# A decoder layer in float32 on one core: queries and gates of the cross attention by seven products, another order of the steps into and out of the experts

## The chip, the core and the metric

The kernel runs on one core of one Trainium2 chip. The metric is the device time of one execution in microseconds (us). The five engines of a core are named as the profile names them: PE (TensorE, with PEld its weight loads), DVE (VectorE), ACT (ScalarE), POOL (GpSimd) and SP (SyncE, which here only issues transfers). PE takes a product of float32 as two instructions.

## What is computed

A decoder layer on x (8 x 112 tokens, 512 wide) and a context (8 x 375 x 512), all float32:

```
x = layernorm(x + self_attention(x))          # 16 heads of 128, causal
q, k = feature_map(x Wq^T), feature_map(ctx Wk^T)   # where(x > 0, x + 1, exp(x))
gate = sigmoid(x Wg^T + bg)
attn = (q . sum(k v)) / (q . sum(k) + 1e-6)    # 16 heads of 32
x = layernorm(x + (attn * gate) Wo^T)
logits = x router^T + bias                     # 8 experts, the top 2 with softmax weights
out = sum over the 2: w_e * (act(x gate_up_e + b) down_e + b)
x = layernorm(x + out)
```

Here act is `(clip(up, -7, 7) + 1) * g * sigmoid(1.702 g)` with `g = min(gate, 7)`.

## The kernel before

Tokens lie in seven tiles of 128 (`xn`), weights in nine slabs of 128 x 4 x 512 (`slab`; three more come for the experts). Up to 445 us the self attention runs: per head, `seven` (L319) makes queries and keys for both halves of the tokens by seven products in place of eight, from sums of tokens (`combine_tokens`, L302, on DVE) and sums of weights (`combine_weights`, L312, on POOL). The products share three PSUM banks, ACT and DVE take intermediate results out between them.

Then come two pairs of context blocks (`project_pair`, L797), the transposes of the tokens (`transposing`, L210) and, from 470 to 518 us, queries and gates of the cross attention (L923 to L942): two weights, four groups of 128 columns, two halves of 448 tokens, four chunks, 64 products. DVE and ACT form the feature map (L261) out of PSUM, ACT the sigmoid. After that `biases` and `more_biases` (L943 to L949) are cleared by POOL, and the sums of the next pair are made there (L788).

The order of the instructions on PE, DVE, ACT and SP is that of the text only inside `manual_schedule` (L478, and L1142 to the end); elsewhere, and always on POOL, a planner orders them by priorities. From L1143 a loop over the 8 batches does the attention (`summarize`, `attend`), and chains of generators lie beside it: `tick()` (L727) moves each chain by one `yield`, `settle(n)` runs them until n are left. `close(t)` (L1045) is such a chain: output projection, normalisation, routing of tile t (`route`, L556), and, for some t, `list_blocks` (L642), which works out which expert each step takes and which block of 128 tokens. `LISTS` (L40) has five lists: steps 0; 1 and 2; 3 and 4; and the two lists of the rest, both after the last tile. Each tile's tokens are scattered to `store` in DRAM by POOL.

18 steps follow (L1366): fetch 128 tokens (`fetch_tokens`, L1031, POOL queue), transpose, two inner products (`products`, L1127, 512 columns each of gate and up), activation (`project`, L1208), transpose, down product (`down`, L1231), result `y` scattered to `parts` in DRAM. `LANES` says in which slabs a step's weights lie; steps 5 to 12 take two half blocks. `fetch_inner`, `fetch_down` issue the weights on the SP queue, behind what that queue waits for; `fetch_biases` (L1014) brings bias rows on the ACT queue (steps 0 and 1: SP) to every 32nd partition, and `spread_biases` (L1026) copies them to the others by `stream_shuffle` on DVE.

The end: after step 12's scatter the two results of each token are read back (L1426, 14 loads on SP), added and normalised by `close_tiles` (L1297). The blocks of the last five steps (`LATE`) are not ready by then: they gather the other result (`gather`, L1273), add their own (`add_own`, L1270, POOL for three of them), and are normalised and written by row numbers (`write`, L1282). Rows that occur in later blocks too are found by `find_again` (L1327), and step 17 takes step 16's rows by a product with a 0/1 matrix (`finish`, L1350).

Of the kernel before, what the change touches and what calls it, by code (L numbers as in the profile page):

```python
# [48 lines left out]
LISTED = [*range(EARLY), *range(10, 18), *range(EARLY, 10)]  # L49
LATE = 5  # L50
# [10 lines left out]
def decoder_layer(ctx: ExitStack, tc: tile.TileContext, t_in: dict, out: bass.AP):  # L61
# [170 lines left out]
    def closing_roots(a: int, b: int):  # L232
        rstd = closing[:, 2, a:b]
        nc.scalar.activation(rstd, closing[:, 1, a:b], AF.Sqrt, bias=eps)
        nc.vector.reciprocal(rstd, rstd)
        nc.vector.scalar_tensor_tensor(
            closing[:, 3, a:b], closing[:, 0, a:b], -1.0, rstd, ALU.mult, ALU.mult
        )
# [48 lines left out]
    with tc.tile_pool(name="att", bufs=2) as att:  # L287
# [14 lines left out]
        def combine_tokens(a: int, b: int):  # L302
# [16 lines left out]
        def seven(name: str, tag: str, w1, w2, ws, cols, turned_: bool, c11, c12, c21, c22):  # L319
# [236 lines left out]
    def route(t: int):  # L556

        x2T = side.tile([P, C, P], F32, tag="x2T", name=f"x2T_{t}")
# [165 lines left out]
    xblk = [side.tile([P, W], F32, name=f"xblk{i}") for i in range(NQ)]  # L724
# [12 lines left out]
    with tc.tile_pool(name="cross", bufs=2) as cr:  # L737
# [179 lines left out]
        wxo = weights("wxo", 0, 8)  # L917
# [5 lines left out]
        for n, w in (("xq", wxq), ("xg", wxg)):  # L923
            for g in range(C):
                for half in range(2):
                    cols = slice(half * HALF, (half + 1) * HALF)
                    ps = bank(f"{n}ps_{g}_{half}")
                    for c in range(C):
                        nc.tensor.matmul(  # L929
                            ps[:, :HALF],  # L930
                            w[:, c, g * P : (g + 1) * P],
                            xT[:, c, cols],
                            start=(c == 0),
                            stop=(c == C - 1),
                        )
                    if n == "xq":
                        tmp = cr.tile([P, HALF], F32, tag="tmp", name=f"qt_{g}_{half}")
                        feature_map(qf[:, g, cols], ps[:, :HALF], tmp)
                    else:
                        nc.scalar.activation(  # L940
                            gate[:, g, cols], ps[:, :HALF], AF.Sigmoid, bias=bg[:, g : g + 1]
                        )  # L942
# [3 lines left out]
        more_biases = side.tile([P, 2 * D], F32, name="more_biases")  # L946
# [67 lines left out]
        def fetch_biases(s: int, queue=nc.scalar, engine=ET.Activation):  # L1014

            for i in range(len(LANES[s])):
                on, half = part_of(s, i)
                e = listed(0, s, half, engine, E - 1)
                for to, of in ((inner_bias(s), gubs), (down_bias(s), t_in["db"])):
                    to_ = to[on.start : on.stop : XH]  # L1020
# [5 lines left out]
        def spread_biases(s: int):  # L1026

            for b in (inner_bias(s), down_bias(s)):
                nc.vector.stream_shuffle(b, b, [0] * XH)  # L1029
# [15 lines left out]
        def close(t: int):  # L1045
# [12 lines left out]
            for i, (n, steps_) in enumerate(LISTS):  # L1058
                if t == n - 1:
                    list_blocks(i)  # L1060
# [66 lines left out]
        def products(s: int, st, k: int):  # L1127

            ps = st["ps", k] = bank(f"gups_{s}_{k}")
            for c in range(C):  # L1130
# [12 lines left out]
        for b in range(B):  # L1143
# [6 lines left out]
            else:  # L1150

                fetch_inner(1, of=(1,))
                for s in range(2):
                    fetch_biases(s, nc.sync, ET.SP)
                fetch_down(1)
                fetch_inner(2)
                sums = summarize(b)
# [4 lines left out]
                products(0, steps[0], 1)  # L1162
                tick()
                steps.append(start(1, cr, "bdkv"))
                spread_biases(0)
                last = close(NT - 1)
                next(last)
                settle(0)
# [3 lines left out]
                products(1, steps[1], 1)  # L1172
# [22 lines left out]
    with tc.tile_pool(name="moe", bufs=2, reuse_waits="tile") as moe:  # L1195
# [12 lines left out]
        def project(s: int, st, k: int):  # L1208

            if s > 1:  # L1210
                products(s, st, k)
# [19 lines left out]
        def down(s: int, st):  # L1231
            ps = bank(f"yps_{s}", "aux")
            for c in range(C):
                for rows_, q in parts_of(s):
# [4 lines left out]
                        start=(c == 0),  # L1239
                        stop=(c == C - 1 and s < STEPS - 1),  # L1240
                    )
            if s == STEPS - 1:
                finish(ps, st)
                return
            y = st["y"]
# [246 lines left out]
```

## Time and profile before

| | |
|---|---|
| median of 3 runs | 957.3 us (953.56 to 959.45) |
| the profiled execution | 954.05 us, span 952.5 us, clock 0.986 |
| queries and gates | 470.15 to 518.26 us |
| first expert product | 702.71 us |
| last down product begins | 927.87 us |
| row writes of the late blocks | 939.91 to 946.18 us |

The page gives the busy time of each engine and the span in 40 slices. In the answers, a line of the timeline has the start, the time in all, the engine, the line in the kernel, the operation, output and input, their shapes, the number of instructions, and in brackets how long the engine was idle before and what released it. A line of the chain has start, length and what ran. A line of the waits has who waited, for whom, the total, how often, and the longest. Several instructions merged into one line show their time together.

### The profile page before, as it was taken

Reading aid. Unit: us, or ns where it says so; the run is one execution under the profiler, and the core shown is the slowest. Engines: PE = TensorE matmul, PEld = TensorE weight load, DVE = VectorE, ACT = ScalarE, POOL = GpSimd, SP = SyncE. Lnnn points to the kernel's source line nnn. Section 1 sums busy time; section 2 is a strip of 40 time slices with the busy share of each in tenths; the row PEclk is TensorE's granted clock in tenths of the full one; section 3 lists DMA queues with packets and bytes.
Section 4 is the critical chain, followed back from the end, with each engine's and each line's share of the span. In section 5 each row is a group of like instructions: output and inputs, shape, how many; then the busy total and the mean of one; then the engine's idle time right before and its main releaser. Section 6 shows DMA issues by size and latency. Waiting matters only on the chain.

```text
span 952.5 us, 11049 instructions
## 1 busy us (share of the span) xinstructions
PE 907.8 (95%) x3915; PEld 463.2 (49%) x3915; DVE 500.7 (53%) x1094; ACT 252.8 (27%) x439; POOL 203.0 (21%) x265
## 2 busy tenths in 40 slices
PE   8999999999999999999999999999998899999981
PEld 4346655664445654664555445455454443334440
DVE  5115451663123551457430567666678765555795
ACT  2213321332102330332322232323323322222232
POOL 3103310311001321302002212222101342222343
PEclk9999999999999999999999999999998999999996
DMA  9998201000221001021100111110476999868943
GB/s 331 378 329 283 89 1 44 1 1 1 72 105 44 1 1 44 1 91 62 33 1 1 33 33 56 54 56 1 167 268 232 394 372 330 299 240 347 380 174 130
DMA packets 34919, 130.48 MB, mean 137 GB/s; under 512 B 3846, under 2 KB 8006, under 8 KB 25136
## 3 DMA queue, kind: packets, MB, share of 16 engines
q1 hardware_dynamic: 29184, 114.06, 32.9%
q0 software_dynamic: 4768, 14.98, 4.4%
q10 hardware_dynamic: 912, 0.74, 0.3%
q8 instruction: 31, 0.51, 0.2%
q14 instruction: 24, 0.20, 0.1%
HBM read 122.02 MB, written 30.06 MB: 160 GB/s over the span
## 4 chain that ended last, share of the span: by engine, by line
PE 77%; DVE 12%; DMA 6%; ACT 2%; issue 2%; POOL 1%; ACTq 0%; POOLq 0%; SPq 0%; DVEq 0%
PE ops L272 10%; PE gups L1132 9%; PE yps L1235 4%; PE zps L456 3%; PE xqps L929 3%; PE xgps L929 3%; PE sps L408 2%; PE xops L272 2%; DVE z L902 2%; PE vps_3a L330 1%; PE vps_2a L330 1%; PE pps L448 1%; PE vps_0a L330 1%; PE vps_1a L330 1%; DMA slab<-in_wg_dram 1%
## 5 line engine op out<-in xcount | busy, mean ns | idle before, releaser
L1132 PE MATMUL gups<-slab,bT 128*64 128x512 f32 (+1 forms) x416 | 131.1, 596 | 0.0
L272 PE MATMUL ops<-slab,zT 128*128 128x512 f32 x224 | 98.1, 593 | 0.0
L1132 PEld LDWEIGHTS gups<-slab,bT 128*64 128x64 f32 (+1 forms) x416 | 47.7, 157 | 66.0 <-issue 64.9
L314 POOL TENSOR_TENSOR ws<-slab 128x256 f32<-128x256 f32 x16 | 12.2, 761 | 275.9 <-PE qk_9c L330 83.0
L1235 PE MATMUL yps<-slab,aT 128*64 128x512 f32 (+1 forms) x208 | 68.2, 605 | 0.9 <-ACT aT L1083 0.9
L272 PEld LDWEIGHTS ops<-slab,zT 128*128 128x128 f32 x224 | 41.9, 190 | 49.3 <-issue 48.6
L1214 DVE TENSOR_TENSOR gu<-gups,biases 128x512 f32<-128x512 f32 x36 | 24.8, 689 | 58.6 <-PE gups L1132 58.6
L1083 ACT COPY aT<-aT_ps 128x512 f32<-128x512 f32 x18 | 10.5, 584 | 131.3 <-PE aT_ps L1079 122.6
L281 DVE TENSOR_TENSOR xn<-xn,ops 128x512 f32<-128x512 f32 x28 | 19.1, 684 | 46.2 <-PE ops L272 46.2
L1235 PEld LDWEIGHTS yps<-slab,aT 128*64 128x64 f32 (+1 forms) x208 | 24.8, 161 | 38.4 <-issue 35.7
L463 DVE COPY zT<-zps 128x448 f32<-128x448 f32 x32 | 20.0, 624 | 39.8 <-PE zps L456 39.8
L456 PEld LDWEIGHTS zps<-pT,v 112*128 112x128 f32 x256 | 33.5, 192 | 12.3 <-issue 11.2
L432 DVE TENSOR_REDUCE nm<-p 112x4 f32<-112x448 f32 x32 | 19.7, 616 | 30.5 <-POOL p L422 30.5
L456 PE MATMUL zps<-pT,v 112*128 112x112 f32 x256 | 33.4, 273 | 0.0
L1248 POOL DMA_INDIRECT parts<-y,nums x16 | 17.2, 1073 | 65.2 <-DVE y L1246 38.8
L272 PE MATMUL xops<-slab,gate 128*128 128x512 f32 x56 | 25.7, 602 | 4.8 <-DVE gate L904 4.8
L1029 DVE STREAM_SHUFFLE biases<-biases 128x1024 f32<-128x1024 f32 (+1 forms) x28 | 29.9, 1103 | 0.0
L618 POOL DMA_INDIRECT store<-xn,rows x14 | 14.4, 1030 | 71.7 <-DVE cmp L660 40.1
L416 ACT ACTIVATE p<-sps 112x448 f32<-112x448 f32 x32 | 17.4, 544 | 45.6 <-PE sps L408 45.6
L408 PE MATMUL sps<-k,q 128*112 128x112 f32 x256 | 28.0, 262 | 0.0
L434 ACT ACTIVATE p<-p 112x448 f32<-112x448 f32 x32 | 18.4, 576 | 33.3 <-DVE p L433 32.2
L408 PEld LDWEIGHTS sps<-k,q 128*112 128x112 f32 x256 | 26.6, 178 | 0.5 <-issue 0.4
(807 smaller groups left out, 1705.2 us busy)
## 6 DMA issues: line engine op xcount, KB each, us to landing
slab<-in_wg_dram SPq DMA_DIRECT2D x26, 1024.0 KB
slab<-in_wu_dram SPq DMA_DIRECT2D x26, 1024.0 KB
slab<-in_wd_dram SPq DMA_DIRECT2D x26, 1024.0 KB
store<-slab SPq DMA_DIRECT2D x8, 1806.0 KB
cT<-in_ctxT_dram SPq DMA_DIRECT2D x8, 750.0 KB
slab<-in_wq_dram SPq DMA_DIRECT2D x4, 1024.0 KB
slab<-in_wk_dram SPq DMA_DIRECT2D x4, 1024.0 KB
slab<-in_wo_dram SPq DMA_DIRECT2D x4, 1024.0 KB
```

Of the source, the lines that this page charges most:

```text
L272: nc.tensor.matmul(ps, aT[:, c, t * P : (t + 1) * P], w[:, c, :], start=(c == 0), stop=(c == C - 1),)
L281: nc.vector.tensor_add(xn[:, t, :], xn[:, t, :], ps)
L330: nc.tensor.matmul(ps[:rows, :n], l[:, c, :], r[:, c, :], start=start and c == 0, stop=c == C // 2 - 1, skip_group_check=not start,)
L408: nc.tensor.matmul(ps[:S, i * S : (i + 1) * S], qk["q"][:, rows], qk["k"][:, rows], start=True, stop=True,)
L432: nc.vector.tensor_reduce(nm, p, AX.X, ALU.max, negate=True)
L456: nc.tensor.matmul(zps[:, i * S : (i + 1) * S], v[:, half * 4 + i, hl * DH : (hl + 1) * DH], pT[:, i * S : (i + 1) * S], start=True, stop= ...
L463: nc.vector.tensor_copy(zT[:, hl, half * HALF : (half + 1) * HALF], zps[:, :HALF])
L929: nc.tensor.matmul(ps[:, :HALF], w[:, c, g * P : (g + 1) * P], xT[:, c, cols], start=(c == 0), stop=(c == C - 1),)
L1029: nc.vector.stream_shuffle(b, b, [0] * XH)
L1132: nc.tensor.matmul(ps[rows_], st["bT"][:, c, rows_], slab[3 * q + k][:, c, :], start=(c == 0), stop=(c == C - 1),)
L1214: nc.vector.tensor_add(a, ps, st["bias"][:, k * I : (k + 1) * I])
L1235: nc.tensor.matmul(ps[rows_], st["aT"][:, c, rows_], slab[3 * q + 2][:, c, :], start=(c == 0), stop=(c == C - 1 and s < STEPS - 1),)
```

## The change

1. Queries and gates use `seven`, with its token sums (`x1s`) in a new tile `tokens` and its weight sums in slab 8. One group gives 128 columns of the queries and of the gates for both halves. The results go to SBUF, and feature map and sigmoid work there in place, the sigmoid for two groups at a time over 896 columns. The load of `wxo` into slab 8 stands after the products.
2. `tokens` holds the four token blocks (`xblk`), `more_biases` and the transposed tile of `route`, which were tiles of their own.
3. Steps 0, 1, 16 and 17 (`SPREAD`) load their bias rows to all 128 partitions and are not spread by DVE. For steps 0 and 1 the loads go behind step 1's down weights and step 2's inner weights on SP.
4. In the last batch, `settle(0)` (routing of tile 5, list 2) stands before `close` of the last tile; lists 3 and 4 come one `yield` later. `products` can do part of its chunks: those of (0, 1), (1, 1) and (2, 1) are cut in two around other work.
5. At the end `close_tiles` begins a step's half sooner and stops at other places, ACT scales all seven tiles, the three additions on POOL move to DVE, the three late blocks are closed before step 17's down product, the product with `same` opens that product's bank, and a block's row write follows its scaling. `find_again` stands after `down`.

```diff
@@
     def closing_roots(a: int, b: int):
         rstd = closing[:, 2, a:b]
         nc.scalar.activation(rstd, closing[:, 1, a:b], AF.Sqrt, bias=eps)
+        yield
...
-        x2T = side.tile([P, C, P], F32, tag="x2T", name=f"x2T_{t}")
+        x2T = tokens[:, NQ * W + 2 * D :].rearrange("p (c n) -> p c n", c=C)
...
-    xblk = [side.tile([P, W], F32, name=f"xblk{i}") for i in range(NQ)]
+    tokens = side.tile([P, NQ * W + 3 * D], F32, name="tokens")
+    xblk = [tokens[:, i * W : (i + 1) * W] for i in range(NQ)]
...
-        wxo = weights("wxo", 0, 8)
+        ws = slab[8].rearrange("p c n -> p (c n)").rearrange("p (i n) -> p i n", i=2)
+        ws = [ws[:, i].rearrange("p (a c n) -> p a c n", a=4, c=C // 2) for i in range(2)]
+        group = [slice(g * P, (g + 1) * P) for g in range(C)]
+        for g in range(2):
+            combine_weights(ws[g], wxq[:, :, group[g]], wxg[:, :, group[g]])
+        x1s = tokens[:, : 4 * T].rearrange("p (a c n) -> p a c n", a=4, c=C // 2)
...
+        combine_tokens(0, HALF, x1s)
+        halves_ = slice(0, HALF), slice(HALF, T)
+        for g in range(C):
+            for _ in seven(
+                f"xqg_{g}", "mm", wxq[:, :, group[g]], wxg[:, :, group[g]],
+                [ws[g % 2][:, i] for i in range(4)], slice(0, HALF), False,
+                qf[:, g, halves_[0]], qf[:, g, halves_[1]],
+                gate[:, g, halves_[0]], gate[:, g, halves_[1]], x1s, x1ends,
+            ):
+                pass
+            if g + 2 < C:
+                combine_weights(ws[g % 2], wxq[:, :, group[g + 2]], wxg[:, :, group[g + 2]])
+            for half, cols in enumerate(halves_):
+                tmp = cr.tile([P, HALF], F32, tag="tmp", name=f"qt_{g}_{half}")
+                feature_map(qf[:, g, cols], qf[:, g, cols], tmp)
+            if g % 2:
+                for i in (g - 1, g):
+                    nc.scalar.activation(
+                        gate[:, i, :], gate[:, i, :], AF.Sigmoid, bias=bg[:, i : i + 1]
+                    )
+        wxo = weights("wxo", 0, 8)
...
-                    to_ = to[on.start : on.stop : XH]
+                    to_ = to[on] if s < SPREAD or s >= STEPS - SPREAD else to[on.start : on.stop : XH]
...
                 if t == n - 1:
+                    if i == 3:
+                        yield
                     list_blocks(i)
...
-                for s in range(2):
-                    fetch_biases(s, nc.sync, ET.SP)
                 fetch_down(1)
                 fetch_inner(2)
+                for s in range(SPREAD):
+                    fetch_biases(s, nc.sync, ET.SP)
...
-                products(0, steps[0], 1)
+                products(0, steps[0], 1, range(2))
                 tick()
+                products(0, steps[0], 1, range(2, C))
                 steps.append(start(1, cr, "bdkv"))
-                spread_biases(0)
+                settle(0)
                 last = close(NT - 1)
                 next(last)
-                settle(0)
                 chains.append(last)
                 products(1, steps[1], 0)
                 tick()
-                products(1, steps[1], 1)
+                products(1, steps[1], 1, range(2))
...
         def close_tiles():
             for t in range(NT):
                 engine = nc.vector if t < 4 else nc.gpsimd
                 engine.tensor_add(xn[:, t, :], xn[:, t, :], seconds[:, t, :])
                 closing_stats(t, xn[:, t, :])
-                if t in (1, 2):
+                if t in (0, 2, 4):
                     yield
+            roots = closing_roots(0, NT)
+            next(roots)
             yield
-            closing_roots(0, NT)
+            for _ in roots:
+                pass
+            yield
             for t in range(NT):
-                closing_scale(t, xn[:, t, :], t > 2)
+                closing_scale(t, xn[:, t, :], True)
                 nc.sync.dma_start(out=out[t * P : (t + 1) * P, :], in_=xn[:, t, :])
-                if t == 2:
-                    yield
+                if t == 1:
                     yield
...
+        def end_steps(*several, by_act=()):
+            for _ in closing_roots(at_close(several[0]), at_close(several[-1]) + 1):
+                pass
+            for s in several:
+                closing_scale(at_close(s), steps[s]["sum"], s in by_act)
+                write(steps[s])
...
             if st:
                 project(s, st, 0)
-                if s < STEPS - 1:
-                    tick()
+                tick()
+                if s == 0:
+                    products(1, steps[1], 1, range(2, C))
+                if s == 2:
+                    products(2, st, 1, range(2))
...
                 gate_sigmoid(s, st)
+                if s == STEPS - 1:
+                    tick()
                 begin_result(s)
...
             if s == STEPS:
+                two = steps[STEPS - 2]
+                ps = before_["begun"] = bank("yps_last", "aux")
+                nc.tensor.matmul(ps, before_["same"], two["y"], start=True, stop=False)
+                three = range(STEPS - LATE, STEPS - 2)
                 settle(0)
-                close_steps(*range(STEPS - LATE, STEPS - 2), by_act=True)
+                for i in three[1:]:
+                    add_own(i)
+                    stats_of(i)
+                add_own(STEPS - 2)
+                end_steps(*three, by_act=three)
+                add_own(STEPS - 1)
+                stats_of(STEPS - 2)
...
-            if STEPS - LATE <= s < STEPS - 1:
-                find_again(s + 1)
-            if s + 1 < STEPS:
+            if 0 < s < STEPS - 1:
                 spread_biases(s + 1)
             if before_:
                 down(s - 1, before_)
+            if STEPS - LATE <= s < STEPS - 1:
+                find_again(s + 1)
             if s == STEPS - 1:
-                for late in steps[STEPS - LATE : STEPS - 2]:
-                    add_own(late, nc.gpsimd)
-                add_own(before_)
-                add_own(st)
-            if before_:
+                add_own(STEPS - LATE)
+                stats_of(STEPS - LATE)
+            if before_ and s < STEPS - 1:
                 if s == STEPS - 3:
                     chains.append(close_tiles())
-                if s != STEPS - 3:
-                    tick()
+                tick()
...
             if s == STEPS:
-                for st in steps[STEPS - LATE :]:
-                    write(st)
+                stats_of(STEPS - 1)
+                end_steps(STEPS - 2, STEPS - 1)
```

## The prediction

> **What bounds the kernel now.** I read the page, the table by stretches, the waits of TensorE, the timeline of the two places where TensorE idles, and the chain of the end. The page, with the DMA share per slice in its last line:
>
> ```profile
> span 952.5 us, 11049 instructions
> ...
> PE 907.8 (95%) x3915; PEld 463.2 (49%) x3915; DVE 500.7 (53%) x1094; ACT 252.8 (27%) x439; POOL 203.0 (21%) x265
> ...
> DMA  9998201000221001021100111110476999868943
> ```
>
> TensorE is busy 95%, so only removed products and its idle stretches pay. The table by stretches (stretch, its length, busy time of PE, PEld, DVE, ACT, POOL, granted clock, DMA share, GB/s):
>
> ```profile
> 470.00:518.00 48.00, 48.00 (x131) 24.40 (x130) 10.86 (x18) 10.83 (x17) 0.00 (x0) 1.00 0.00 0
> ...
> 720.00:740.00 20.00, 16.69 (x50) 8.78 (x48) 17.42 (x90) 7.07 (x12) 4.36 (x5) 0.83 0.81 315
> 740.00:760.00 20.00, 17.03 (x53) 8.51 (x53) 14.21 (x33) 8.58 (x14) 8.12 (x9) 1.00 1.01 393
> 780.00:800.00 20.00, 20.00 (x88) 7.00 (x84) 11.36 (x24) 3.23 (x6) 6.70 (x9) 1.00 1.01 372
> ...
> 905.00:925.00 20.00, 18.45 (x55) 8.66 (x52) 19.23 (x45) 4.64 (x8) 7.50 (x8) 1.00 0.47 176
> 925.00:952.50 27.50, 5.95 (x16) 2.16 (x14) 14.62 (x27) 8.53 (x14) 11.06 (x10) 0.71 0.38 134
> ```
>
> Three places count: the queries and gates, 48 us of TensorE alone; the passage into the expert steps, 6.3 us idle at 720 to 760 with VectorE busy; the end, where VectorE has 19.23 of 20 us. The waits of TensorE (total, times, longest):
>
> ```profile
> PE aT_ps L1079 <- DVE gu L1223: 5.7, 3, 3.0
> ...
> PE yps L1352 <- DVE y L1246: 1.9, 1, 1.9
> PE keys L1332 <- DVE sums L1392: 1.6, 1, 1.6
> ```
>
> VectorE is what TensorE waits for. The timeline shows why at the end:
>
> ```profile
> 927.61 2.50 POOL L1271 TENSOR_TENSOR sums<-sums,y 128x512 f32<-128x512 f32 x2
> 927.61 3.74 DVE L236 SCALAR_TENSOR_TENSOR closing<-closing 128x7 f32<-128x7 f32 x1
> ```
>
> L236 on 128x7 takes 3.74 us; its two later runs took 0.16. It ends at 931.35, as GpSimd's three additions do (930.05 + 1.27): VectorE stood still while GpSimd added. The chain of the end:
>
> ```profile
> 935.09 3.74 DMA out_dram<-xn
> ```
>
> The last tile is written at 935.09 and lands at 938.83. Then GpSimd issues five row writes, 939.91 to 946.18, 1.3 us apart, and 6.3 us later the span ends.
>
> **The sum's base.** The profiled execution took 954.05 us (span 952.5). The median shown is 957.3, 3.25 more (runs 953.56 to 959.45). I work against 954.05 and add half of that, 1.6, at the end.
>
> **A, queries and gates: -3.7.** Removed: 64 products of 448 columns, each two instructions at a pitch of 0.376 us (470.15 to 518.26), 48.1 us. Added: four groups of seven products in two chunks, 56 x 0.752 = 42.1. That is -6.0. The new helpers: L307 to L310 on VectorE (0.62 for 448 columns, so some 1.1 each for 896). The transposed tokens are whole at 471.05; the second sum is ready at 473.2, when the first four products end (470.15 + 3.0): cover exact. The weight sums are 4 x 0.73 per group on GpSimd, idle for 80.6 us there; the first two groups come early, the others lie beside 10.5 us of products, as do a group's four evictions on ScalarE (0.53 each) and five operations on VectorE (0.43 to 0.62). Inside a group the third eviction stands between two products on one bank; in the same pattern at L352 a weight load waits 0.2 us, because the next group's product is put between (vps_1a at 223.96 stands between two of vps_0a): +0.2 x 4 = 0.8. At the stage's end ScalarE has, after the last product, an addition (0.6) and a minimum (0.4) on VectorE ahead, then one exponential 0.6, a table load 1.28 and two sigmoids of 896 columns, some 1.1 each: free 5.4 us on, while the eviction that kvps_2a waits for was issued 2.2 us on and needed 4.5 us on: +1.5. GpSimd's third memset (0.98, earlier at 427) comes into the same gap, covered by that wait. -6.0 + 0.8 + 1.5 = -3.7. Ends: -6.0 (all hidden); +2.0 (no filler, 4 x 0.9, second and third table load in the way, 2.6, and the wait 1.8). I take the value near the vps rows, the same code. The load of wxo moves behind the last product on SP; it has until 552.85, and the context load issued behind it at 531.7 loses nothing.
>
> **B, into the expert steps: -4.7.** From 708.46 TensorE does gups(0,1), lps, bT, xops, cps, gups(1,0), x2T, gups(1,1), lps, cps, aT, bT, yps(0), gups(2,0), aT, bT, gups(2,1): by their pitches (3.43 for eight, 0.44 for a transpose, 0.8 for lps) 28.7 us. It took 39.0 (to 747.44): 10.3 lost, namely 1.5 on cps, 1.8 and 3.0 on gu, 2.9 at a half clock (yps 731.03 to 736.5 in place of 3.43) and the rest in steps of tenths. New order on VectorE: both shuffles of steps 0 and 1 go (2.05 each: 1.29 + 0.73), route(5) and its list come ahead of tile 6's normalisation. List 2 then ends at 718.2 in place of 723.1; tile 6 is normalised at 720.9 (719.56); gu of step 0 at 727.9 (729.1); step 1's gate at 731.0, the two long lists (5.4 less 1.1 of L675, blocked as L236 was) to 735.3, gu of step 1 at 738.4 (743.0). TensorE: half of gups(1,1) covers lps, half of gups(2,1) covers gu(1). Left: 0.5 on cps(5), 2.1 on gu(0), 0.95 as aT's copy stands behind tile 6's exponential on ScalarE, 1.7 at a half clock, 0.4 small. gups(2,1) ends at 742.7: -4.7. Weights: the loads of step 3 follow list 2 on SP (723.75 to 718.8) and fill a DMA queue idle from 711.5 to 723, so the stream moves by the same 4.8; step 1's down load and step 2's loads go ahead of the two bias loads on SP, which land at some 708 and are needed at 721. Lists 3 and 4 end only 1.1 earlier, but their loads queue behind seven others. GpSimd: the scatter of tile 5 goes 5 us sooner, so tokens(3) do. Ends: -7.3 (no half clock, no copy wait); 0 (the weights hold it).
>
> The half clock in this trace came at 539.84 after a wait of 2.05 us, for 3.41 us, and at 727.6 for 6.83 us; so I let 2.1 us of idling cost 1.7, half of such a window. The Trainium skill, "TensorE: Matmul & The Clock Gate", section "HAM oscillation", only speaks of idle gaps over some 3.4 us; by that rule the 1.7 would not be lost and B would be -6.4.
>
> **C, the end: -5.2.** VectorE between step 16's first gate and step 17's: 17.7 us (905.04 to 922.7) loses step 17's shuffles 2.05, and tile 0 goes ahead (1.56) into the room of step 16's shuffles: gate of 17 at 920.4, gu at 923.6 (926.24). keys go behind yps on TensorE, so 1.6 goes and yps(16) ends at 923.8. ScalarE: root of seven at 919.3 (aT(16) behind it), sigmoid 922.1, two scales, two copies to 925.0, aT(17) 925.6, five scales at 0.73 to 929.25 (934.32). That is 5.1 sooner for the last tile's write, landing at 933.7; five row writes follow from 934.8 at 1.28 to 941: the span's end moves by 5.1 to 5.2. Beside it on VectorE: three additions (0.67) from GpSimd and five statistics, to 934.3; the last scale at 936.0 is needed by the fifth write at 939.9. So the writes are late next, and -8.0 is their end if the write of the tiles does not hold them; -2.5 if VectorE alone sets it (gu's 2.6).
>
> **D, whole bias rows for four steps: +0.3.** 128 rows of 6 KB for 4 or 8 KB: 0.77 MB a step, 2 us at 380 GB/s. For steps 0 and 1 the queue idles. Those of 16 and 17 go ahead of 14 loads of tiles on SP and of the down weights issued at 901.34, landing 905.7; yps(15) now wants them at 909.3: +0.3, ends 0 and +4.
>
> Sum: -3.7 - 4.7 - 5.2 + 0.3 = -13.3, so 940.8 beside 954.05; with the 1.6, **942.4**.
>
> **The rivals.** R1, the weights hold B: DMA share 1.0 from 740 to 800, and yps waited 1.0 us for a down load at 817.25. For: lists 3 and 4, said to come sooner, are put off by one tick and gain only 1.1 us. Against: queue idle until 723. Time 942.4 + 4.7 = 947. R2, A gives nothing: the planner spends it on table loads and bank waits: 946. R3, the change's end gains nothing, since ScalarE's root of seven waits for tiles 5 and 6, whose additions GpSimd may put behind four gathers (922.28 to 927.6) that wait for a scatter; then aT(16) is copied at 931 in place of 920 and C is +6.5: 942.4 + 11.7 = 954. Against: the three additions ran at 900.66 and 905.16. R4, slower: the token blocks, the transposed tile and biases are now one tile; if a load into one part waits for readers of the others, the prefetch goes and each of 13 steps waits some 3 us of the 8 us landing: 942.4 + 39 = 981; over 1.8 us a step it is slower than before by 1%. Against: the biases tile has its parts loaded and read at once (load at 793.73, shuffle of another part at 795.94).
>
> **How the numbers follow.** As forecast 0.50 (936 to 947); R1 0.17, R2 0.13, R3 0.14, R4 0.06. A measurement of this kernel can tell about 1%, 947.7 to 966.9, from no change. Faster: 0.50 + 0.12 + 0.09 = 0.71; same: the rest of R1 and R2, 0.09, and R3 less 0.02, 0.12: 0.21; slower 0.08. The range runs from the good ends (A -6.0, B -7.3, C -8.0, D 0: 934.4) to R3 (954), cut to 934 to 953.
>
> **What would show it.** Products xqg of 42 us and kvps_2a beside them; list 2 at some 5 us after bT(1); no wait of keys; no GpSimd addition L1271; L236 at 0.16; the last tile written some 5 us after step 17's yps begins; row writes 1.3 apart. It is wrong if wd or wg loads appear among TensorE's waits, if aT waits for ScalarE, or if the first row write waits for a scale and not for a tile.

## The result and the profile after

The changed kernel took 945.9 us (median of 4 runs, 942.5 to 949.5) beside 956.7 us for the kernel before: ratio 0.989, 95% interval 0.986 to 0.9925, so it is 10.8 us faster (7 to 13 by the interval). The forecast was 942.4 us, the range 934 to 953. Measured a second time on another occasion (experiment after_again) it took 944.2 us, ratio 0.989 (0.9857 to 0.9921).

The page of the changed kernel; its profiled execution took 949.54 us, the span is 948.0:

```profile
span 948.0 us, 11057 instructions
...
PE 908.9 (96%) x3899; PEld 462.2 (49%) x3899; DVE 506.2 (53%) x1094; ACT 273.2 (29%) x463; POOL 213.1 (22%) x278
...
DMA  8978201000041000011100211010477999768964
```

TensorE has 16 instructions (8 products) fewer and is busy 1.1 us longer, since this execution began at half clock until 13.6 us, the kernel before only until 4.5; in the repeat TensorE is busy 902.1 us. The table by stretches, with the columns as before:

```profile
470.00:518.00 48.00, 47.33 (x143) 24.15 (x142) 22.82 (x37) 25.07 (x36) 6.62 (x8) 1.00 0.00 0
720.00:740.00 20.00, 16.75 (x51) 9.09 (x50) 15.99 (x71) 9.81 (x14) 5.05 (x6) 0.83 0.97 379
740.00:760.00 20.00, 20.00 (x60) 9.82 (x59) 15.48 (x33) 5.75 (x10) 5.82 (x8) 1.00 1.01 365
905.00:925.00 20.00, 17.67 (x43) 7.82 (x42) 18.04 (x39) 7.41 (x11) 9.23 (x9) 0.91 0.55 224
925.00:948.00 23.00, 6.73 (x19) 2.74 (x17) 11.94 (x25) 9.57 (x15) 8.43 (x8) 0.72 0.45 161
```

Two things to see. From 720 to 760 TensorE now idles 3.25 us where it idled 6.3, all of it ahead of 740 and at a granted clock of 0.83. From 905 to 925 VectorE is nearly as full as before (18.04 of 20; 19.23 before) and TensorE idles more (2.3; 1.55 before). The waits of TensorE show by whom:

```profile
PE aT_ps L1107 <- DVE gu L1253: 3.3, 1, 3.3
PE yps L1265 <- DMA slab<-in_wd_dram: 2.3, 1, 2.3
...
PE kvps_2a L815 <- POOL biases L798: 1.9, 1, 1.9
```

Of the three waits for gu one is left, keys no longer wait, and step 15's down load is there, which was not. The end of the chain:

```profile
902.92 7.34 DMA slab<-in_wd_dram
910.40 5.37 PE yps L1265 x8
...
927.79 3.54 ACT xn L245 x5
931.35 2.79 DMA out_dram<-xn
```

The order of the end is the one forecast (TensorE's last product, five scales on ScalarE, the last tile's write, row writes), but it comes late, and behind a down product that ran at 5.37 us in place of 3.60.

**Where the time went.** To compare kernels I cut the span at five marks on TensorE: the first transposes of x1T, the first kvps_10a, the first gups, yps of step 1 (at 746.50 here), yps of step 14 (896.51), the end. The columns are differences of these times in each kernel's trace; the last two are the median of all its runs and its ratio to the kernel before, measured beside it.

| kernel | to x1T | to kvps_10a (A) | to gups | to yps 1 (B) | to yps 14 | to the end (C, D) | span | median | ratio (interval) |
|---|---|---|---|---|---|---|---|---|---|
| before | 467.1 | 198.5 | 37.1 | 44.7 | 150.5 | 54.5 | 952.5 | 956.7 | 1 |
| after | 471.7 | 194.1 | 38.8 | 41.9 | 150.0 | 51.5 | 948.0 | 945.9 | 0.989 (0.986-0.9925) |
| after again | 467.0 | 192.4 | 37.1 | 41.5 | 150.9 | 52.4 | 941.3 | 944.2 | 0.989 (0.986-0.992) |
| e1 | 467.6 | 198.3 | 37.1 | 41.3 | 149.8 | 51.6 | 945.7 | 947.6 | 0.994 (0.992-0.996) |
| e2 | 467.1 | 192.4 | 38.8 | 42.1 | 149.2 | 51.5 | 941.0 | 944.3 | 0.9905 (0.9885-0.992) |
| e3 | 466.8 | 194.1 | 38.8 | 41.5 | 149.7 | 51.7 | 942.5 | 943.8 | 0.9905 (0.988-0.993) |
| e4 (of before) | 467.3 | 196.6 | 37.1 | 44.9 | 150.7 | 55.2 | 951.7 | 953.9 | 0.9994 (0.997-1.0015) |
| e5 | 467.4 | 194.1 | 37.1 | 46.6 | 150.4 | 52.3 | 947.8 | 949.3 | 0.993 (0.9915-0.995) |
| e7 | 467.3 | 192.4 | 38.8 | 39.5 | 150.7 | 52.9 | 941.6 | 943.6 | 0.988 (0.984-0.991) |
| e8 | 466.8 | 194.1 | 38.8 | 42.0 | 149.9 | 51.6 | 943.2 | 944.3 | 0.988 (0.9855-0.990) |
| e9 | 467.4 | 194.1 | 38.8 | 41.6 | 150.7 | 52.2 | 944.7 | 943.8 | 0.987 (0.985-0.989) |
| e10 | 466.9 | 194.1 | 38.8 | 40.9 | 149.7 | 52.0 | 942.3 | 943.3 | 0.987 (0.984-0.991) |
| b1 | 466.9 | 194.1 | 38.8 | 39.6 | 150.7 | 51.5 | 941.5 | 943.8 | 0.987 (0.984-0.990) |
| b3 | 468.7 | 194.1 | 38.8 | 39.3 | 150.7 | 51.4 | 943.0 | 942.6 | 0.986 (0.983-0.989) |

The columns "to kvps_10a" and "to gups" hold chance: in each of them a window of 3.41 us at half clock (granted clock 0.5) falls or does not, worth 1.7 us (see the last section). Without it the change is A -4.2 to -4.4, B -2.8 to -3.3, the middle between -0.5 and +0.4, the end -2.1 to -3.0. That makes -9 to -11; the medians show -10.8, and -11.5 in the repeat (944.2 beside 955.7). Medians of kernels this close can't be told apart (their intervals are 4 to 7 us wide), so the experiments are read stage by stage.

### The profile page after: what moved, and what is told of

It reads as the page before. It is cut to its first block, busy times and chain, and to the rows that moved or that the text cites. A ratio compares the mean times of both kernels' runs of the same rounds, so it can differ in the third digit from the quotient of the medians.

```text
span 948.0 us, 11057 instructions
## 1 busy us (share of the span) xinstructions
PE 908.9 (96%) x3899; PEld 462.2 (49%) x3899; DVE 506.2 (53%) x1094; ACT 273.2 (29%) x463; POOL 213.1 (22%) x278
## 4 chain that ended last, share of the span: by engine, by line
PE 79%; DVE 10%; DMA 5%; ACT 2%; POOL 2%; issue 1%; SPq 0%; POOLq 0%; ACTq 0%; DVEq 0%
PE ops L274 10%; PE gups L1162 10%; PE yps L1265 5%; PE zps L460 3%; PE sps L412 2%; PE xops L274 2%; DVE z L907 2%; DMA biases<-in_db_dram 2%; PE vps_3a L334 1%; PE vps_2a L334 1%; PE vps_1a L334 1%; PE pps L452 1%; PE vps_0a L334 1%; DMA slab<-in_wg_dram 1%; PE kvps_2a L815 1%
## 5 line engine op out<-in xcount | busy, mean ns | idle before, releaser
L1162 PEld LDWEIGHTS gups<-slab,bT 128*64 128x64 f32 (+1 forms) x416 | 46.6, 157 | 64.7 <-issue 64.5
L1265 PE MATMUL yps<-slab,aT 128*64 128x512 f32 (+1 forms) x200 | 65.4, 614 | 2.3 <-DMA slab<-in_wd_dram 2.3
L274 PEld LDWEIGHTS ops<-slab,zT 128*128 128x128 f32 x224 | 41.9, 190 | 49.3 <-issue 49.1
L1244 DVE TENSOR_TENSOR gu<-gups,biases 128x512 f32<-128x512 f32 x36 | 24.8, 690 | 59.0 <-PE gups L1162 58.9
L274 PE MATMUL xops<-slab,gate 128*128 128x512 f32 x56 | 25.8, 604 | 4.8 <-DVE gate L909 4.8
L907 DVE RECIPROCAL z<-z 128x448 f32<-128x448 f32 x8 | 23.6, 2953 | 0.3
```

Of the source, the lines that this page charges most:

```text
L274: nc.tensor.matmul(ps, aT[:, c, t * P : (t + 1) * P], w[:, c, :], start=(c == 0), stop=(c == C - 1),)
L907: nc.vector.reciprocal(zf, zf)
L1162: nc.tensor.matmul(ps[rows_], st["bT"][:, c, rows_], slab[3 * q + k][:, c, :], start=(c == 0), stop=(c == C - 1),)
L1244: nc.vector.tensor_add(a, ps, st["bias"][:, k * I : (k + 1) * I])
L1265: nc.tensor.matmul(ps[rows_], st["aT"][:, c, rows_], slab[3 * q + 2][:, c, :], start=(c == 0 and s < STEPS - 1), stop=(c == C - 1),)
```

## The experiments

**e1, A undone.** The 64 plain products of the kernel before stand again in place of the seven-product groups.

```diff
-        for g in range(C):
-            for _ in seven(f"xqg_{g}", ...)
+        for n, w in (("xq", wxq), ("xg", wxg)):
+            for g in range(C): ...   # the 64 products of before
```

> The changed kernel with part A alone undone: queries and gates by the 64 plain products of 448 columns again. Theory (A is worth 4.45 us: products 4.3 shorter, its new wait and half clock 2.0 and 0.15, against 2.1 lost at the same place before): 945.9 + 4.4 = 950.3 us, ratio to the kernel before 0.994; the 64 products take 48.1 us and the next product waits for no memset of GpSimd. Rival (R2, A gives nothing, since what it wins is taken back by weights that come no sooner): 946 us, ratio 0.989, with the first expert products starting at the same distance from the load that feeds them.

947.6 us, ratio 0.994, as the theory had it. The A column goes back to 198.3, and nothing later takes the difference back, so R2 falls. The waits of e1 also show the trade inside A: kvps_2a's wait for GpSimd (1.9) is gone, and an old wait is back.

```profile
PE sumps L869 <- DVE kf L829: 1.8, 1, 1.8
```

**e5, B undone.** Lists, splits, fetch order and shuffles of steps 0 and 1 as before.

```diff
-                    if i == 3:
-                        yield
...
-                products(0, steps[0], 1, range(2))
-                tick()
-                products(0, steps[0], 1, range(2, C))
+                products(0, steps[0], 1)
+                tick()
                 steps.append(start(1, cr, "bdkv"))
-                settle(0)
+                spread_biases(0)
```

> The changed kernel with part B alone undone: list 3 is not put off by a tick, the products of steps 0 to 2 are not split, the biases of steps 0 and 1 are loaded to every 32nd row, ahead of step 1's down weights, and spread by VectorE. Theory (B is worth 2.8 us): gu(1) makes TensorE wait some 3 us again, list 2 ends 5 us later, yps of step 1 begins 2.8 us later against the last product of the queries, and the time is 945.9 + 2.8 = 948.7 us, ratio 0.992. Rival (R1, the weights take B back by 823 us): yps of step 1 begins later, but the down load that the product at 817 to 823 waits for comes at the same time as in the changed kernel, and the time is 946 us.

949.3 us. The B column is 46.6, 4.7 to 5.1 more than in the two traces of the changed kernel and the same distance is kept to step 14 (150.4), so the weights take nothing back and R1 falls. It is more than the 2.8 expected, and more than the 44.7 of the kernel before: this trace has a half-clock window at 740.25 that the kernel before had not (1.7); the remaining 0.2 I can't place. The old wait for gu(1) is there again:

```profile
PE aT_ps L1105 <- DVE gu L1251: 5.4, 2, 3.6
```

**e4, on the kernel before: who stops L236?** One word of the kernel before is changed.

```diff
-                    add_own(late, nc.gpsimd)
+                    add_own(late, nc.vector)
```

> The kernel before with one word changed: its three late additions run on VectorE and not on GpSimd. Theory (VectorE stands still while GpSimd adds): L236 on 128x7 takes 0.16 in place of 3.74 us, the three additions cost VectorE 3 x 0.67 = 2.0, so VectorE is free 1.6 us sooner and the end comes 1 to 1.6 us sooner: 955.3 us, ratio 0.9985. Rival (L236 was slow for a reason of its own): L236 still takes over 3 us and the time is 956.7 + 2.0 = 958.7 us.

953.9 us, ratio 0.9994 (0.997 to 1.0015): no change. But L236 answers the question. With three additions beside it it took 3.74 us; now one is left beside it, GpSimd's y addition, and the two lines of the timeline are:

```profile
928.54 1.28 POOL L1268 TENSOR_TENSOR y<-y,biases 128x512 f32<-128x512 f32 x1
928.55 1.30 DVE L236 SCALAR_TENSOR_TENSOR closing<-closing 128x7 f32<-128x7 f32 x1
```

An operation of 0.16 us lasts as long as the addition on the other engine. So the cause was read rightly, but removing it is not the whole gain of the end: VectorE pays for the additions what it is spared, and the end column is 55.2 beside 54.5.

**e7, the same cause in the middle.** The changed kernel's lines at the passage into the expert steps:

```profile
728.15 1.92 DVE L1249 TENSOR_SCALAR gu<-gu 128x512 f32<-128x512 f32 x1
728.51 1.27 POOL L1295 TENSOR_TENSOR y<-y,biases 128x512 f32<-128x512 f32 x1
...
731.52 1.12 PE L1107 MATMUL aT_ps<-ident,gu 128*128 128x128 f32 x4 [3.25 <-DVE gu L1253]
```

L1249 takes 0.43 elsewhere. GpSimd adds the bias to step 0's result in the middle of it, at the only place of this passage where TensorE waits long for VectorE. The kernel before has no such addition there, and its L1219, the same operation, takes 0.43. e7 puts that addition, and step 1's, on VectorE just ahead of the down product's addition.

```diff
-            nc.gpsimd.tensor_add(y, y, bias)
+            if s > 1:
+                nc.gpsimd.tensor_add(y, y, bias)
...
             y = st["y"] if s < STEPS - 1 else st["sum"]
+            if s < 2:
+                nc.vector.tensor_add(y, y, down_bias(s))
```

> The changed kernel with the bias additions of the results of steps 0 and 1 taken from GpSimd and put on VectorE, just ahead of the addition of the down products. Theory (B fell short because VectorE stood still while GpSimd added: L1249 took 1.92 and 1.74 in place of 0.43 us): L1249 takes 0.43 both times, gu(0) is ready 1.5 us sooner, the wait of aT(0) is 1.8 in place of 3.25 us, and the time falls by 1.5 us, by up to 3 if the half clock after that wait is one window in place of two: 943 to 944.4 us. Rival 1 (L1249 is slow for another reason): it still takes 1.9 us, no change. Rival 2 (R1, the weights hold the passage): the wait goes but comes back before 823 us at a down load, no change.

```profile
722.11 0.51 DVE L1249 TENSOR_SCALAR gu<-gu 128x512 f32<-128x512 f32 x1
...
724.06 0.77 PE L1107 MATMUL aT_ps<-ident,gu 128*128 128x128 f32 x4 [1.83 <-DVE gu L1253]
```

As the theory said: L1249 at 0.51 and 0.43, the wait 1.83 in place of 3.25, one half-clock window in place of two (the repeat of the changed kernel has one as well). The B column falls from 41.5-41.9 to 39.5; of these 2.0 to 2.4 us the middle gives back at most 0.7 (150.7). The time is 943.6 us, in the range expected, but it is within the scatter of the repeat.

The Trainium skill, "SBUF — State Buffer", section "Who interferes with whom", states a rule for such lines: a VectorE instruction with two inputs in SBUF contends with a GpSimd instruction that reads SBUF, and so does one in a mode that uses both of VectorE's port pairs; the one issued first holds the shared ports for its whole length, and the other stands still. L236 has two inputs in SBUF and agrees with it. L1249 has one input and takes 0.43 us free, where a two-input operation of its size takes 0.69, which fits such a mode. Additions with one input in PSUM agree too: L1244 took 0.68 us beside a GpSimd addition in e8, at 905.85.

**e2 and e3, D.** Step 15's down product waits 2.33 us for its weights. What SyncE waited for before it issued that load, 860 to 915 us of the changed kernel:

```profile
...
SPq L1473 <- DMA parts<-y,nums: 5.3, 1, 5.3
SPq L1473 <- DMA biases<-gubs: 4.5, 1, 4.5
SPq L1473 <- DMA biases<-in_db_dram: 2.5, 1, 2.5
```

L1473 loads the closing tiles; the down load stands behind it. It waits 5.3 us for a scatter of results and 7.0 for bias loads. e2 takes the whole bias rows of steps 16 and 17 away, e3 puts the down load ahead of the tiles.

```diff
-                    to_ = to[on] if s < SPREAD or s >= STEPS - SPREAD else to[on.start : on.stop : XH]
+                    to_ = to[on] if s < SPREAD else to[on.start : on.stop : XH]
```

```diff
             if before_:
+                fetch_next(s - 1, fetch_down)
                 if s == PAIRED:
                     ...   # the 14 loads of tiles
-                fetch_next(s - 1, fetch_down)
```

> The changed kernel with the biases of steps 16 and 17 loaded to every 32nd row and spread by VectorE again, as before the change; those of steps 0 and 1 stay whole. Theory (the whole rows hold the transfers that SyncE's loads of tiles and of step 15's down weights queue behind, worth 4.2 us): the wait of 2.33 us of step 15's yps and its half clock (5.37 in place of 3.6 us) go, SyncE no longer waits for bias loads, and the two shuffles of 2.05 us come back, that of step 17 on the path: 945.9 - 4.2 + 2.0 = 943.7 us. Rival (the down weights are late because they stand behind 14 loads of tiles on SyncE, whatever the biases do): yps of step 15 still waits some 2 us, and the time is 945.9 + 2.0 = 948 us.

> The changed kernel with the down weights of steps 15 and 16 issued ahead of the 14 loads of tiles on SyncE. Theory: step 15's down load is issued some 9 us sooner, its wait of 2.33 us and the half clock after it (1.8) go, and the tiles, 2 MB of weights later, are still whole before the root of seven is due at 920: 945.9 - 4 = 942 us. Rival: the tiles, now behind the weights, come some 5 us later, the root of seven is late and the copy of aT(16) behind it on ScalarE makes TensorE wait: 946 us or more.

In both the wait is gone, so the whole rows do delay the load (SyncE issues it 3.3 us after step 14's yps in e2, 6.4 after it in the changed kernel). But neither moved the end: 51.5 and 51.7 us from step 14 on, beside 51.5 to 52.4 with the wait. The medians, 944.3 and 943.8, look like the 943.7 and 942 that I expected only because the base was 944 to 946 and not 945.9 flat. My theory that D cost 4.2 us falls: a late load of 2.3 to 2.4 us costs nothing there (e1 has it too, 51.6); with 4.1 to 4.3 us of waiting (e5, e7, the repeat) the stretch is 52.3 to 52.9, some 1 us longer. Something else ends at the same time. In e3 it looks like this:

```profile
907.47 2.03 DVE L1253 SCALAR_TENSOR_TENSOR gu<-gu,gu 128x512 f32<-128x512 f32 x1
907.65 1.29 POOL L1328 TENSOR_TENSOR xn<-xn,seconds 128x512 f32<-128x512 f32 x1
...
915.68 0.66 DVE L1244 TENSOR_TENSOR gu<-gups,biases 128x512 f32<-128x512 f32 x1
915.80 0.30 ACT L235 ACTIVATE closing<-closing,eps 128x7 f32<-128x7 f32 x1 [12.90 <-DVE closing L231]
...
916.62 5.10 PE L1265 MATMUL yps<-slab,aT 128*128 128x512 f32 x8 [2.91 <-ACT aT L1111]
```

ScalarE's root of seven (L235) waits for VectorE's last statistics, the copy of aT(16) stands behind it in ScalarE's order, and TensorE waits 2.91 us for that copy and then runs at half clock. (In e2 it waits 3.31 us at the same place.) VectorE itself has no gap from 898.5 to 916.7; its first work on step 17's gate (L1244, 915.68) comes 6 us after its products ended, and GpSimd's tile additions stop it again (2.03 for 0.69).

**e8, e9: the root, and VectorE standing still.** Both stand on e3. e8 puts the root behind aT(16)'s copy; e9 puts the additions of tiles 4 to 6 on VectorE.

```diff
             for t in range(NT): ...
+            yield
             roots = closing_roots(0, NT)
...
-                tick()
+                if s < STEPS - 1:
+                    tick()
...
                 before_["aT"] = transposed_block(f"aT_{s - 1}", before_["g"], moe, "aT")
+                if s == STEPS - 1:
+                    tick()
+                    tick()
```

```diff
-                engine = nc.vector if t < 4 else nc.gpsimd
-                engine.tensor_add(xn[:, t, :], xn[:, t, :], seconds[:, t, :])
+                nc.vector.tensor_add(xn[:, t, :], xn[:, t, :], seconds[:, t, :])
```

> The changed kernel with the down weights ahead of the tile loads, as in the run that gave 943.8 us, and ScalarE's root of the seven tiles put behind the copy of aT(16) in place of ahead of it. Theory (curing the late down weights won nothing net, since aT(16) then stood 2.9 us behind the root, which waits for VectorE's statistics of tiles 5 and 6; the gate of step 17 stands behind the same root): the wait of 2.9 us and its half clock go, yps of step 16 begins 2.9 us sooner, but the sigmoid of step 17 does not move, so aT(17) comes only some 1.1 us sooner: 942.7 us. Rival (the root is not what sets the end): yps sooner, and the time falls by all of 2.9 + 1.5, to 939.4. Third: the end does not move at all, 943.8, since the scales of the tiles on ScalarE and the writes set it.

> The changed kernel with the down weights ahead of the tile loads, and the closing additions of tiles 4 to 6 on VectorE in place of GpSimd. Theory (VectorE is the end's bound, and each GpSimd addition of 1.28 us stops one of its instructions for about as long: 2.03 for 0.69, 1.25 for 0.15, 1.16 for 0.28): VectorE pays 3 x 0.69 = 2.1 and is spared some 3.3, so the root of the seven tiles, the copy of aT(16) behind it and the end come 1 to 1.3 us sooner: 942.6 us. Rival (the tiles' loads set the root): VectorE then waits for the loads of tiles 5 and 6 where GpSimd waited before, everything behind it is late, and the time is 944 to 946 us.

e8: yps of step 16 begins 3.4 us sooner against step 14 (22.4 us after it, 25.8 in e3), and aT(17) waits 3.62 us in its place; the end column is 51.6, so the third reading holds: the end does not move. e9: the end column is 52.2; VectorE stands still less, but its first tile addition now waits 0.85 us for a load and it pays 2.1 for the additions. The theory of e9 falls.

**e10, is VectorE's tile work the bound at all?** On e3, additions and statistics of tiles 4 to 6 left out.

```diff
+    nc.gpsimd.memset(closing, 1.0)
...
-                engine = nc.vector if t < 4 else nc.gpsimd
-                engine.tensor_add(xn[:, t, :], xn[:, t, :], seconds[:, t, :])
-                closing_stats(t, xn[:, t, :])
+                if t < 4:
+                    nc.vector.tensor_add(xn[:, t, :], xn[:, t, :], seconds[:, t, :])
+                    closing_stats(t, xn[:, t, :])
```

> The changed kernel with the down weights ahead of the tile loads, and with the additions and statistics of the closing left out for tiles 4, 5 and 6 (they are scaled by constants and written all the same). Theory (VectorE's closing of the tiles is what holds the root of seven, the gate of step 17 behind it, and so what C lost against its forecast): VectorE is spared 2.6 us of statistics and some 3.3 of standing still, its first operation on step 17's gate, 6 us after its products in the kernel with the tiles, follows its products at once, no wait for aT(16), and the end comes 3 to 5 us sooner than 943.8: 939 to 941 us. Rival (the loads of the tiles or the writes set the end): less than 1 us sooner, 943 us.

```profile
907.85 0.30 ACT L236 ACTIVATE closing<-closing,eps 128x7 f32<-128x7 f32 x1 [4.87 <-DVE closing L232]
...
912.72 3.60 PE L1266 MATMUL yps<-slab,aT 128*128 128x512 f32 x8
...
917.27 1.28 POOL L1303 DMA_INDIRECT sums<-parts,others  x1 [2.36 <-DMA parts<-y,nums]
...
921.82 2.35 DVE L1299 TENSOR_TENSOR sums<-sums,y 128x512 f32<-128x512 f32 x1 [3.17 <-DMA sums<-parts,others]
...
925.80 0.69 DVE L1299 TENSOR_TENSOR sums<-sums,y 128x512 f32<-128x512 f32 x1 [0.68 <-DMA sums<-parts,others]
...
929.83 1.04 POOL L1313 DMA_INDIRECT out_dram<-sums,places  x1 [6.22 <-ACT sums L246]
```

Half of the theory holds: the root comes 7.5 us sooner (17.5 after step 14's yps, 25.0 in e3), TensorE no longer waits for aT(16), and the scales of the tiles are done at 920.9 (926.3 in e3). And the end column is 52.0. A third chain is now seen to run beside the other two: GpSimd's scatters of steps 13 to 15 (906.96, 910.40, 913.82 here), the four gathers that wait for the last of them (917.27 to 921.37), and VectorE's additions of the late blocks, which idle until the gathered rows land. The first row write is at 929.83, 39.5 us after step 14's yps; in e3 it was at 930.04, 39.2 us after it.

**b1 and b3, the cures together.** b1 is e7 and e3 in one; b3 adds e8 and moves the start of step 17's result and two more scales ahead on ScalarE.

```diff
                 if s == STEPS - 1:
+                    begin_result(s)
                     tick()
                     tick()
...
-                if t == 1:
+                if t == 3:
                     yield
```

> The changed kernel with two cures together: the bias additions of steps 0 and 1 on VectorE, and the down weights ahead of the tile loads. From the traces of the two alone: the passage into the expert steps 2.4 us shorter (of which 0.7 was given back at a down load by the middle steps), the stretch from step 14's yps to the end the same 51.7 us as in all kernels with the new end: 942.2 us. Rival (the two late down loads were one and the same shortage, and it comes back elsewhere): no better than either alone, 943.7 us.

> Both cures, and on ScalarE in step 17: the copy of aT(16), then the two copies of the result's start (0.71 each), then the root of the seven tiles, the sigmoid, four scales, the copy of aT(17), three scales. Theory (ScalarE is full from the root to the last tile's scale, and the row writes wait for that tile's write): the two copies leave that stretch, the last tile is written 1.4 us sooner and the span ends 1.4 us sooner than with the cures alone: 940.8 us. Rival (VectorE sets the end: the late sums are its work until 931): no change, 942.2 us, and the first row write waits for a scale of the sums and not for a tile's write.

943.8 and 942.6 us, ratios 0.987 (0.984 to 0.990) and 0.986 (0.983 to 0.989); the changed kernel beside them had 0.989 (0.986 to 0.992). The intervals overlap, so no version is shown to be faster than the changed kernel, though in their traces the passage is 1.9 to 2.6 us shorter. In b3 the scales were done sooner and the write of the last tile took longer, 4.72 us beside 2.79, and the end column is 51.4. The first row write, at 930.47, came 1.1 us after that write had landed:

```profile
924.68 4.72 DMA out_dram<-xn
```

**The changed kernel again.**

> The changed kernel as it is, once more. If the slow start of its profiled execution (half clock until 12.9 us, 4.6 us later than the kernel before at the transposes of the second attention) was chance, as in nine of ten traces so far the transposes began at 466.8 to 467.6 us, they begin at 467 us here and the span is about 943.5 us; the ratio to the kernel before is 0.988 to 0.990. If the start belongs to the changed kernel, the transposes begin at 471 us again.

944.2 us, span 941.3 in the profile. The slow start was chance. The first products of the program, in the changed kernel's first trace and in the repeat:

```profile
7.40 3.76 PE L334 MATMUL vps_0a<-slab,x0T 128*112 128x512 f32 x4 [0.78 <-DVE x0T L223]
```

```profile
6.87 1.97 PE L334 MATMUL vps_0a<-slab,x0T 128*112 128x512 f32 x4 [0.78 <-DVE x0T L223]
```

The same four products at half clock and at full. x1T's transposes begin at 466.8 to 467.6 us in twelve of the fourteen traces, at 468.7 and 471.7 in two.

## Why the prediction was right, and where its sum was not

The direction, the places and the order of the parts were right; the sum was too large: -13.3, where the medians show -10.8 and -11.5 and the marks -9 to -11. Of the 3.5 us between 942.4 and 945.9, 1.0 is the base (the kernel before had 956.7, the forecast took 955.65) and 2.5 the sum. Two terms were too large: B took too short a wait for gu(0), and C priced one chain of the end where others end with it. Two of the three signs that the prediction named as showing it wrong came: wd and wg loads among TensorE's waits (2.3 and 0.4 us), and a first row write that waits for a scale and not for a tile. That the time still fell into the range is in part luck: the wd load cost next to nothing, and A gave 0.5 to 0.7 us more than forecast for a reason that the forecast did not have.

- **A, forecast -3.7, measured -4.2 to -4.4.** The group's products took 43.8 us net of the kvps_2a in between (474.77 to 520.27, less 1.72), with one wait of 0.67; the forecast had 42.1 and 0.8, and the other 1.0 us lies in small steps between products. The wait at the stage's end was 1.90 (forecast 1.5), but for GpSimd's sums for the next pair (L798), which stand behind its memsets, and not for ScalarE. A wait of 2.1 us that the kernel before had at sumps went with it; the forecast had not counted that. e1 shows that all of A arrives at the end, so R2 falls.
- **B, forecast -4.7, measured -2.8 to -3.3.** List 2, step 1's gate and the splits did what was said: bT(1) at 714.63, list 2 done at 719.8; the wait for gu(1) went. The term that failed is "2.1 on gu(0)": it was 3.0 to 3.3, since L1249 took 1.92 in place of 0.43 beside GpSimd's y addition. The forecast used this effect for L236 at the end and for L675 and did not ask which other VectorE instruction a GpSimd addition meets. e7 shows that this is it. The 1.7 for a half clock was right in kind; in the first trace two windows came in a row. (In the trace of the kernel before the granted clock falls at 540.43 and 728.16, not at 539.84 and 727.6 as the prediction has it; no term depends on that.) R1 falls by e5.
- **C, forecast -5.2, measured with D -2.1 to -3.0.** L236's successor takes 0.17 us, the keys' wait is gone, the row writes are 1.3 us apart (once 1.55). No run takes C back alone; its size is read from the end column. The steps that failed are the times of VectorE's list: root of seven at 919.3, gate of step 17 at 920.4. Against step 14's yps the root came 24.2 us on (920.70 - 896.51), forecast 21.3 (919.3 - 898.0), and at 25.0 in e2 and e3. The forecast added VectorE's instructions at their free durations and left out what GpSimd's tile additions stop: 3.0 us in the changed kernel (1.28 for 0.43, 1.17 for 0.69, 1.84 for 0.15). But e10 shows that VectorE's list is not the only bound: without it the scatters, the gathers and the late sums end at the same time. "The writes are late next" was the wrong successor: the last tile had landed at 934.14, and the first row write followed at 935.21, when the first late sum was scaled. The lines of the changed kernel:

```profile
909.34 1.84 DVE L1121 TENSOR_TENSOR is_first<-tokens,es 128x1 f32<-128x1 f32 x1
...
909.86 1.29 POOL L1328 TENSOR_TENSOR xn<-xn,seconds 128x512 f32<-128x512 f32 x1
...
920.70 0.30 ACT L235 ACTIVATE closing<-closing,eps 128x7 f32<-128x7 f32 x1 [11.65 <-DVE closing L231]
...
935.21 1.04 POOL L1312 DMA_INDIRECT out_dram<-sums,places  x1 [6.62 <-ACT sums L245]
```

- **D, forecast +0.3, ends 0 and +4.** The wait that the prediction feared is there (2.33 us, half clock behind it), and it costs nothing, as e2 and e3 show, up to about 1 us when it grows over 4. From the trace alone I would have said 4.2.
- **R3** (ScalarE's root holds aT(16)) is there in a weak form, 2.5 to 3.3 us in e2, e3, e9 and b1, and not for GpSimd's order behind gathers. **R4** (one tile, false waits) shows nowhere: step 1 to step 14 takes 150.0 and 150.9 us in the two traces of the changed kernel, 149.2 to 150.7 in the experiments on it, beside 150.5.

What stays open is how far the end would fall if all three chains were shortened at once, and what holds GpSimd's first scatter in e3 and e10 until 906: the tile loads read the table that it writes, but the profile names a load of weights. Neither was tried.

## What to carry to other kernels

Where GpSimd has elementwise work, look at which VectorE instruction it will lie beside: the addition's whole 1.28 us is put on that instruction, and that matters where another engine waits for it. Before a stall is priced, ask what else ends at the same time: here a visible wait of 2.3 us with a half clock behind it was worth nothing; another chain was seen to end with it, and an experiment that only leaves work out (e10) found the third. Compare kernels that differ by a few us by marks inside the trace, since each of the clock's windows at 520 and 670 us alone moves the time by 1.7 us.

## What the runs showed of the hardware

- **Half clock.** All windows between the start and the last 20 us are 3.41 us long or twice that. They began during or just after waits of TensorE of 1.75 us and more (one, e5's at 723.18, after a wait of 1.47), but such a wait did not always bring one: after kvps_2a's wait of 1.90 us one came in 8 of the 11 kernels that have it, after kvps_10a's of 2.02 in 9 of 14. The table shows it as 1.7 us more or less in two columns. The Trainium skill, "TensorE: Matmul & The Clock Gate", section "HAM oscillation", speaks of idle gaps over some 3.4 us; here 1.83 us (e7) and 1.75 us (b3) were enough, and the measurement decides. What decides between a window and none can be read from the traces: in each, the windows start on one grid of 3.41 us, and in 44 of 45 cases TensorE had been busy less than half of the grid's stretch just before (0.49 at most; once 0.57). Only 4 stretches under half (0.43 to 0.48) were followed by none. So the same wait counts or not by how the grid cuts it.
- **GpSimd and VectorE.** VectorE instructions of 0.15 to 0.75 us took up to 2.4 when a GpSimd addition of 1.28 lay beside them, also when VectorE's was recorded as begun 0.36 us earlier (728.15 and 728.51 above); who was first can't be read from the recorded starts. Down to 128x1 operands: L1121 took 1.84 us at 909.34 in the changed kernel, 0.15 in e2.
